# Moving the pieces of a block's end to other frames in a two-layer graph attention kernel

## The chip, the cores and the metric

The kernel runs on one core of one Trainium2 chip. Such a core has five engines with queues of their own: TensorE (matmuls; PE in the profile, its weight loads PEld), VectorE (DVE), ScalarE (ACT), GpSimd (POOL) and SyncE (SP), which issues most DMAs. The metric is the time of one execution on the device in microseconds, lower is better; the figure compared is the median of several runs.

## The reference

Input is x (8 batches, 2048 nodes, 256 features) and an adjacency matrix (2048 x 2048, 0 or 1). All arithmetic is 32-bit floating point. Two layers follow each other, each with a layer norm and a relu ahead of it and a residual around it.

- Layer 0: h = relu(norm(x)); q, k, v are projections of h, 4 heads of 64. The 2048 keys are split into 8 chunks of 256. Logits are clipped to -10 and 10, set to -10 where there is no edge, and the softmax is taken **within each chunk**; the 8 results are added. Then comes an output projection, plus h as residual, a layer norm with gamma and beta, and x is added.
- Layer 1: h = relu(norm(x)) W; the attention logit of nodes i and j is leaky_relu(src_i + dst_j), masked by the edges, with a softmax over all 2048; relu of the weighted sum of h, added to x.

## The kernel before, in words

**Tiling.** The queries of a batch are split in 4 blocks of 512 (nb = 0 to 3, in the code also zero, low, mid and last). A step is one block with one chunk of 256 keys, so a batch has 32 steps, 8 to a block. In a step TensorE makes the logits of 4 head tiles (L411), VectorE clips them and applies the edges in one instruction (clip, L451), ScalarE takes the exponential (L460), GpSimd adds two halves of the exponentials (add, L466), TensorE sums them over the keys (sums, L439) and multiplies the exponentials with v (values, L427). ScalarE turns the sums into 1/sum by a logarithm and an exponential (invert, L471 and L472), VectorE multiplies the numerators by it (scale, L481, into ctxT in a block's first step and into `prod`, of one buffer, in the others), and a DMA issued by GpSimd adds prod to ctxT (gather, L486).

**Frames.** The order of all instructions is written out by hand, and every engine runs its own in that order. A loop over frames f = 2 to 34 puts parts of four steps side by side: in frame f the logits of step f-1, the values of steps f-2 and f-3, the sums of step f-2, the scaling and gather of step f-3. A frame has two halves, `begin` and `end`, numbered n = 2f and 2f+1. Other work is hung into half frames as pieces: `todo[n]` lists what goes with n. Pieces without a mark run late: those of an even n in `end`, after clip 2 and **before** exponentials 1 and 2; those of an odd n in the same `end`, **after** these exponentials, just before the next frame begins with invert. Pieces marked first, pe, pe1 or mid have places of their own. SyncE's queue also holds the no-ops (`fence`) that order two groups of matmuls in one bank.

In what follows the frame of a step is the time from the first sums matmul of that step to that of the next step; it holds the end of one loop frame and most of the following one. A piece at n = 2f is issued around the sums of step f-2.

**A block's end.** When the 8 steps of block nb are done, `Between` makes the block's output. `beside()` gives its pieces with offsets from the block's end, n = (nb+1) x 16 + offset, for blocks 0, 1 and 2; block 3 comes at the end of the attention, outside of `beside()`. The pieces: `load` fetches x of the block (SP, 512 KB, L153); `residual` makes relu(norm(x)) again for two tiles (2 ScalarE ops, L293, tag hn, five buffers); `bias` adds bo to it (GpSimd, L665); `output_tiled` is the projection on TensorE (L635), `take_tiles` adds the residual (VectorE, L650); `stats` are mean and variance of one tile of 128 rows (VectorE, L270 and L271); `power` makes 1/sqrt (3 small ScalarE ops, L275 to L277), `shift` multiplies it by the mean (GpSimd, L281), `scaled` applies both to four tiles (4 ScalarE ops, L679); `gamma` and `beta` multiply and add (GpSimd, L685, L689); `add` adds the result to x (GpSimd, L693). After that `stats1`, `power1`, `shift1` do the norm of layer 1. Pieces with offsets of 16 and more stand beside early pieces of the next block.

**Around it.** In batch 0 the frames also hold the rest of the adjacency (8 searches on VectorE, L213, and conversions on ScalarE, L231, whose int tiles share the tag of x, four buffers). In the last frames of a batch the next batch's projections begin. Between the attentions of two batches TensorE runs layer 1 of the one and the projections of the other (L865, L355, L369).

Of the kernel before, what the change touches and what calls it, by code (L numbers as in the profile page):

```python
# [28 lines left out]
def gnn_two_layers(  # L29
# [26 lines left out]
    TB = NB // P  # L56
    NNB = N // NB
# [101 lines left out]
    def first(piece):  # L159

        piece.kind = "first"
        return piece

    def pe(piece):

        piece.kind = "pe"
        return piece

    def pe1(piece):
        piece.kind = "pe1"  # L170
        return piece

    def mid_clips(piece):
        piece.kind = "mid"
        return piece
# [418 lines left out]
    class Between:  # L594
# [150 lines left out]

        def beside(self):

            todo = {
                -3: [self.load],
                3: [lambda: self.residual(0)],  # L750
                4: [lambda: self.residual(1)],
                5: [lambda: self.bias(0)],
                6: [lambda: self.bias(1)],
                8: [pe(lambda: self.output_tiled(0)), lambda: self.stats([0]), lambda: self.beta(0)],
                9: [
                    pe1(lambda: self.output_tiled(1)), mid_clips(lambda: self.take_tiles(0)),
                    mid_clips(lambda: self.take_tiles(1)), lambda: self.stats([1]),
                ],
                10: [lambda: self.stats([2]), lambda: self.beta(1)],
                11: [lambda: self.stats([3])],  # L760
                12: [self.power],
                13: [self.shift],
                14: [lambda: self.scaled(range(TB))],
                15: [lambda: self.gamma(0)],
                16: [lambda: self.gamma(1)],
                18: [lambda: self.add(0)],
                20: [lambda: self.add(1)],
            }

            def at(n, *pieces):  # L770
                todo.setdefault(n, []).extend(pieces)

            if self.nb == NNB - 2:
                return todo
            at(22, lambda: self.stats1([0]))

            at(25, first(lambda: self.stats1([1, 2, 3])))
            at(26, self.power1)
            at(27, self.shift1)
            if self.nb == 1:  # L780
                at(28, lambda: self.norm1(0))
                at(29, lambda: self.norm1(1))
            return todo
# [501 lines left out]
```

The softmax here doesn't subtract the row's maximum and nothing guards it: scores larger than these inputs give would overflow.

## Time and profile before

| what | value |
|---|---|
| median of 3 runs | 3623.25 us (3621.5 to 3624.46) |
| the profiled execution: time | 3624.46 us |
| the profiled execution: span | 3622.7 us |
| TensorE clock granted | 0.998 |
| attention of one batch (from the first step's sums to the last's) | 251.4 to 264.0 us |
| from there to the next batch's first sums | 187.0 us in all but one case |

| group | count | mean ns |
|---|---|---|
| clip, L451 DVE | 1024 | 1220 |
| exponential, L460 ACT | 1024 | 1050 |
| add, L466 POOL | 512 | 2406 |
| scale, L481 DVE into prod | 448 | 685 |
| 1/sum, L471 and L472 ACT | 256 each | 597 and 630 |
| residual of blocks, L293 ACT, from x and krn | 128 | 586 |
| scaled, L679 ACT | 128 | 588 |
| bias L665, gamma L685, beta L689, add L693, POOL | 64, 48, 64, 48 | 1522, 1578, 1563, 1569 |
| gather, L486 POOL | 224 | 859, and 4.8 us (median) to its landing |

An instruction is named by its line, its engine and the tiles that it writes and reads. A row of the timeline has the start and the length in us; "x2" joins two instructions of one kind. What stands in square brackets is how long the engine was idle before, and whose signal ended that. A chain of instructions that ended last is part 4 of the page; part 3 lists the DMA queues with packets, megabytes and share. Two ScalarE ops that follow each other overlap a little, so that two residual ops take 1.06 us and four of L679 take 2.06.

### The profile page before, as it was taken

What the parts mean: (1) busy time and instruction counts of PE and PEld (TensorE: products, weight loads), DVE (VectorE), ACT (ScalarE), POOL (GpSimd) and SP (SyncE); (2) the same over time, 40 slices, a digit from 0 to 9 for tenths busy, and PEclk for the clock granted to TensorE, in tenths of its full rate; (3) what the DMA queues carried; (4) which work ended last, traced back from release to release, by engine and by line L of the source; (5) the groups of instructions that cost most, each with busy time, mean ns of one, the idle gap of its engine ahead of it and who ended that gap; (6) DMA issues with size and microseconds to landing.
All of it is one profiled execution on the core that took longest, in us unless ns stands there. A gap on an engine that the chain in (4) does not pass through costs nothing.

```text
span 3622.7 us, 104823 instructions
## 1 busy us (share of the span) xinstructions
PE 3587.4 (99%) x46544; PEld 2202.7 (61%) x46544; DVE 2580.6 (71%) x3967; ACT 1960.9 (54%) x2975; POOL 1788.1 (49%) x1138
## 2 busy tenths in 40 slices
PE   8999999999999999999999999999999999999999
PEld 4444785547744577555775558744586455865568
DVE  5887577866777667786677766677576785757866
ACT  5677416774167732676326772367723677137650
POOL 0678016870178702786027850378503784047831
PEclk9999999999999999999999999999999999999999
DMA  6444213341133412343113432144322343114321
GB/s 223 114 109 100 49 56 84 84 107 35 64 81 83 107 35 68 84 96 83 53 50 84 104 74 62 48 85 99 71 61 59 78 96 73 53 48 92 75 60 44
DMA packets 149431, 283.62 MB, mean 78 GB/s; under 512 B 39664, under 2 KB 104944, under 8 KB 140784
## 3 DMA queue, kind: packets, MB, share of 16 engines
q0 software_dynamic: 32256, 117.45, 17.6%
q1 hardware_dynamic: 100080, 157.36, 13.5%
q8 instruction: 364, 5.96, 0.7%
q10 hardware_dynamic: 16640, 2.10, 0.4%
q14 instruction: 91, 0.75, 0.1%
HBM read 138.41 MB, written 21.02 MB: 44 GB/s over the span
## 4 chain that ended last, share of the span: by engine, by line
PE 96%; DMA 2%; ACT 1%; DVE 1%; issue 0%; POOL 0%; ACTq 0%; SPq 0%; DVEq 0%; POOLq 0%
PE ps_s L411 24%; PE ps_n L427 24%; PE ps_s L865 12%; PE ps_t L439 6%; PE ps_n L865 6%; PE ps_t L865 6%; PE ps_t L635 2%; PE ps_t L355 2%; PE ps_n L355 2%; PE ps_s L355 2%; PE ps_t L723 2%; PE ps_n L723 1%; PE ps_t L369 1%; PE ps_n L369 1%; PE ps_t L302 1%; DMA ctxT<-prod 1%
## 5 line engine op out<-in xcount | busy, mean ns | idle before, releaser
L466 POOL TENSOR_TENSOR both<-e 128x1024 f32<-128x1024 f32 x512 | 1217.8, 2406 | 641.1 <-PE ps_t L439 353.3
L451 DVE SCALAR_TENSOR_TENSOR e<-ps_s,bound 128x1024 f32<-128x1024 f32 x1024 | 1223.9, 1220 | 401.4 <-PE ps_s L411 398.6
L411 PE MATMUL ps_s<-q,k 64*32 64x512 f32 x16384 | 1435.0, 590 | 2.1 <-DVE e L451 2.1
L460 ACT ACTIVATE e<-e 128x1024 f32<-128x1024 f32 x1024 | 1050.5, 1050 | 524.8 <-DVE e L451 505.1
L427 PE MATMUL ps_n<-e,v 64*32 64x512 f32 x16384 | 1220.2, 590 | 2.7 <-ACT e L460 2.1
L427 PEld LDWEIGHTS ps_n<-e,v 64*32 64x32 f32 x16384 | 453.9, 107 | 476.4 <-issue 396.4
L411 PEld LDWEIGHTS ps_s<-q,k 64*32 64x32 f32 x16384 | 451.8, 106 | 472.0 <-issue 326.9
L883 POOL TENSOR_TENSOR x<-x,r 128x256 f32<-128x256 f32 x124 | 95.8, 773 | 1107.2 <-DVE rz L875 1000.7
L439 PE MATMUL ps_t<-both,ones 64*32 64x512 f32 x4096 | 534.7, 591 | 0.1
L865 PE MATMUL ps_s<-g,w 128*128 128x257 f32 x2048 | 448.5, 380 | 0.0
L865 PEld LDWEIGHTS ps_s<-g,w 128*128 128x128 f32 x2048 | 389.4, 190 | 56.5
L481 DVE TENSOR_TENSOR prod<-ps_n,rz 128x512 f32<-128x512 f32 x448 | 288.3, 685 | 159.3 <-PE ps_n L427 96.4
L848 DVE SCALAR_TENSOR_TENSOR w<-bound,w 128x1024 f32<-128x1024 int8 x256 | 313.7, 1225 | 8.7
L865 PE MATMUL ps_n<-g,w 128*128 128x257 f32 x1024 | 292.4, 382 | 0.0
L865 PE MATMUL ps_t<-g,w 128*128 128x257 f32 x1024 | 289.8, 380 | 0.0
L842 DVE TENSOR_SCALAR w<-src,cd 128x512 f32<-128x512 f32 x512 | 265.2, 560 | 10.7 <-ACT src L836 6.9
L471 ACT ACTIVATE rz<-ps_t 128x512 f32<-128x512 f32 x256 | 152.8, 597 | 175.7 <-PE ps_t L439 136.9
L486 POOL DMA_DIRECT2D ctxT<-prod x224 | 192.3, 859 | 57.7 <-DVE prod L481 55.2
L865 PEld LDWEIGHTS ps_n<-g,w 128*128 128x128 f32 x1024 | 192.8, 190 | 44.3 <-issue 17.6
L865 PEld LDWEIGHTS ps_t<-g,w 128*128 128x128 f32 x1024 | 193.8, 189 | 28.2
L275 ACT ACTIVATE krn<-mv,eps 128x4 f32<-128x4 f32 x32 | 9.5, 296 | 292.7 <-DVE mv L271 292.7
L439 PEld LDWEIGHTS ps_t<-both,ones 64*32 64x32 f32 x4096 | 115.2, 106 | 85.8 <-SPq L383 42.4
(126 smaller groups left out, 3005.0 us busy)
## 6 DMA issues: line engine op xcount, KB each, us to landing
ctxT<-prod POOLq DMA_DIRECT2D x224, 512.0 KB, 4.8
bound<-bound_d SPq DMA_DIRECT2D x62, 1024.0 KB, 5.7
xp<-in_x_dram SPq DMA_DIRECT2D x60, 512.0 KB, 5.7
rows<-in_adj_dram SPq DMA_DIRECT2D x32, 512.0 KB, 5.2
x<-in_x_dram SPq DMA_DIRECT2D x32, 512.0 KB, 4.6
out_dram<-x SPq DMA_DIRECT2D x31, 512.0 KB, 2.9
src<-source_d SPq DMA_DIRECT2D x24, 256.0 KB, 4.8
bound_d<-bound_part ACTq DMA_DIRECT2D x16, 128.0 KB, 4.4
```

The costliest lines, as they stand in the source:

```text
L355: nc.tensor.matmul(pp, w[:, di, do * P:(do + 1) * P], self.hT[nb][:, di, :], start=di == 0, stop=di == FC - 1,)
L411: nc.tensor.matmul(self.s[n, o][c * Q:(c + 1) * Q, kt, :], self.k[p][rows, at:at + Q], self.q[p][rows, nb * NB:(nb + 1) * NB], start=True, ...
L427: made.append(nc.tensor.matmul(self.num[n, c][h * Q:(h + 1) * Q, :], self.v[rows, j * KT + kt, at:at + Q], self.e[n, p][rows, i * KT + kt, :],
L439: nc.tensor.matmul(self.total[n][h * Q:(h + 1) * Q, :], ones[rows, :], self.both[n, h // 2][rows, h % 2, :], start=half == 1, stop=half == 0,)
L451: nc.vector.scalar_tensor_tensor(self.e[n, p][:, i * KT:(i + 1) * KT, :], self.s.pop((n, o)), -CLIP * SC, bounds[nb][:, j * KT:(j + 1) * K ...
L460: nc.scalar.activation(e, e, AF.Exp, scale=1.0 / SC)
L466: nc.gpsimd.tensor_tensor(self.both[n, p], e[:, 0], e[:, 1], op=ALU.add)
L481: nc.vector.tensor_tensor(dst[:, c, :], self.num.pop((n, c)), self.rz[n], op=ALU.mult)
L486: nc.gpsimd.dma_start(self.ctxT[nb], self.prod.pop(n), accum_op=ALU.add)
L842: nc.vector.tensor_scalar(w[:, i, :], self.src[nb], self.cd[:, 0, j:j + 1], self.cd[:, 1, j:j + 1], op0=ALU.mult, op1=ALU.max,)
L848: nc.vector.scalar_tensor_tensor(two, bounds1[nb][:, j - 1:j + 1, :], 0.0, two, op0=ALU.is_gt, op1=ALU.mult)
L865: nc.tensor.matmul(accs[t][:, 0:F + 1], w[:, i, t * P:(t + 1) * P], g[:, j, :], start=j == 0, stop=j == NT - 1,)
```

## The change

Only the table of `beside()` is edited, the offsets at which pieces are hung into the half frames. x is loaded 6 half frames earlier; the two residual pieces go from 3 and 4 to -6 and -5, the two bias pieces from 5 and 6 to -4 and -2. The fourth tile of statistics, power, shift and scaled and the first gamma go one half frame later each. The second gamma goes from 16 to 18 and the two adds from 18 and 20 to 20 and 22; in block 2 (`soon`), whose end meets the end of the attention, they go to 17, 18 and 20. output_tiled, take_tiles, beta and the norm of layer 1 stay.

```diff
         def beside(self):
 
+            soon = int(self.nb == NNB - 2)
             todo = {
-                -3: [self.load],
-                3: [lambda: self.residual(0)],
-                4: [lambda: self.residual(1)],
-                5: [lambda: self.bias(0)],
-                6: [lambda: self.bias(1)],
+                -9: [self.load],
+                -6: [lambda: self.residual(0)],
+                -5: [lambda: self.residual(1)],
+                -4: [lambda: self.bias(0)],
+                -2: [lambda: self.bias(1)],
                 8: [pe(lambda: self.output_tiled(0)), lambda: self.stats([0]), lambda: self.beta(0)],
                 9: [
                     pe1(lambda: self.output_tiled(1)), mid_clips(lambda: self.take_tiles(0)),
                     mid_clips(lambda: self.take_tiles(1)), lambda: self.stats([1]),
                 ],
                 10: [lambda: self.stats([2]), lambda: self.beta(1)],
-                11: [lambda: self.stats([3])],
-                12: [self.power],
-                13: [self.shift],
-                14: [lambda: self.scaled(range(TB))],
-                15: [lambda: self.gamma(0)],
-                16: [lambda: self.gamma(1)],
-                18: [lambda: self.add(0)],
-                20: [lambda: self.add(1)],
+                12: [lambda: self.stats([3])],
+                13: [self.power],
+                14: [self.shift],
+                15: [lambda: self.scaled(range(TB))],
+                16: [lambda: self.gamma(0)],
+                18 - soon: [lambda: self.gamma(1)],
+                20 - 2 * soon: [lambda: self.add(0)],
+                22 - 2 * soon: [lambda: self.add(1)],
             }
```

## The prediction

> **What bounds the kernel now.** I read the page first, then the attention stretches one by one, then the timelines of the engines inside one frame. In this page's first and fourth part and its list of queues, TensorE is busy all the time and carries the chain; the third line is used further down.
>
> ```profile
> PE 3587.4 (99%) x46544; PEld 2202.7 (61%) x46544; DVE 2580.6 (71%) x3967; ACT 1960.9 (54%) x2975; POOL 1788.1 (49%) x1138
> ...
> q8 instruction: 364, 5.96, 0.7%
> ...
> PE 96%; DMA 2%; ACT 1%; DVE 1%; issue 0%; POOL 0%; ACTq 0%; SPq 0%; DVEq 0%; POOLq 0%
> ```
>
> A change that moves no TensorE work can only alter how long TensorE stands still. Its matmuls are pipelined, so such stops don't show as idle time; they show as longer frames. The next lines are busy times by stretch for the attention of batches 1 to 6, from the first matmul of the first step's row sums to that of the last (columns: window, length, busy time of PE, PEld, DVE, ACT, POOL, clock, DMA).
>
> ```profile
> 549.22:805.65 256.43, 256.43 (x4832) 128.22 (x4820) 198.50 (x237) 183.64 (x243) 200.35 (x118) 1.00 0.40 92
> 992.69:1251.79 259.10, 258.97 (x4833) 127.99 (x4821) 198.51 (x237) 184.30 (x243) 200.54 (x118) 1.00 0.40 91
> 1438.81:1694.68 255.87, 255.87 (x4833) 128.89 (x4820) 198.58 (x237) 184.18 (x243) 200.45 (x118) 1.00 0.41 92
> 1886.50:2143.07 256.57, 256.30 (x4833) 129.70 (x4820) 198.77 (x237) 183.86 (x243) 200.60 (x118) 1.00 0.41 92
> 2330.10:2588.44 258.34, 258.12 (x4833) 127.78 (x4821) 198.47 (x237) 183.68 (x243) 200.24 (x118) 1.00 0.40 91
> 2775.46:3034.08 258.62, 258.62 (x4832) 128.43 (x4820) 198.61 (x237) 184.38 (x243) 200.29 (x118) 1.00 0.40 91
> ```
>
> The same work takes 255.87 to 259.10 us. Against the shortest, the six lose 0.56 + 3.23 + 0 + 0.70 + 2.47 + 2.75 = 9.7 us. A clean frame is 7.72 us (the sums' first matmul at 646.54, then at 654.27 and 661.99). All that shorter stops could give, with batches 0 and 7 and about 1 us left in the best batch, is some 20 us of 3623.
>
> What makes the losses? Frame by frame, nearly every long one has a late scaling of the numerators on VectorE (prod, L481). One clean frame, and two in which it waits (start, length, idle before and releaser):
>
> ```profile
> 658.36 1.29 DVE L481 TENSOR_TENSOR prod<-ps_n,rz 128x512 f32<-128x512 f32 x2
> ...
> 577.70 1.29 DVE L481 TENSOR_TENSOR prod<-ps_n,rz 128x512 f32<-128x512 f32 x2 [1.01 <-DMA ctxT<-prod]
> ...
> 1029.80 1.29 DVE L481 TENSOR_TENSOR prod<-ps_n,rz 128x512 f32<-128x512 f32 x2 [1.35 <-DMA ctxT<-prod]
> ```
>
> prod has one buffer, and the accumulating DMA of the step before ("gather", L486) still reads it. Measured from the frame's mark (its first sums matmul), the scaling ends at +5.38 in the clean frame, +6.51 and +6.75 in the others; those two frames are 0.58 and 0.83 us too long. So TensorE stops when the scaling ends after about +5.93; the slack is 0.55 us. The gather is issued at +7.1 and lands 4.5 to 6.7 us later.
>
> Is a late issue, from GpSimd pieces, to blame? The two pieces of one frame, on GpSimd:
>
> ```profile
> 677.50 1.58 POOL L693 TENSOR_TENSOR x<-x,o 128x512 f32<-128x512 f32 x1
> 678.75 1.57 POOL L665 TENSOR_TENSOR hn<-hn,bo_r 128x512 f32<-128x512 f32 x1
> 680.00 5.02 POOL L466 TENSOR_TENSOR both<-e 128x1024 f32<-128x1024 f32 x2
> 684.71 1.55 POOL L665 TENSOR_TENSOR hn<-hn,bo_r 128x512 f32<-128x512 f32 x1
> ```
>
> The adds end at 685.0, about 0.1 us later than in other frames, and no gather follows: this is the block's first step, which writes ctxT directly. The doubled frame costs nothing; its frame is 7.72 us. With one piece GpSimd idles 0.84 us before the adds. In the frames after the first stop of a block the gather starts at +7.05 to +7.15, pieces or not: the lateness is in the transfer.
>
> **What the Trainium skill says.** "DMA: Bandwidth & Descriptors", section "Queues, rings and completion order": each DMA engine takes turns between its queues, a packet at a time. "Perfetto Trace Analysis", section "The 4-stage abstract model": an instruction has 64 bytes. The trace agrees: (46544 + 46544) x 64 B = 5.96 MB, the instruction queue's total in 364 packets of 16 KB. These are TensorE's instructions. In batch 3 the gathers that landed in 4.5 us had mostly no such packet in their window; the one of 6.7 us at 1031.4 has one, and no packet of a load. The program as built has 24068 TensorE instructions before and after, so these collisions stay in their frames. "PSUM — Partial Sum Buffer", section "Engine vs sequencer instructions": the queues of ScalarE, VectorE and GpSimd are strict FIFO; the timelines agree, so a moved piece delays all behind it.
>
> **The change, part by part.** It concerns three block ends in each of 8 batches, 24 in all; no instruction's work is added or removed.
>
> *x load (L153), SP, three frames earlier.* It was issued 1.3 us into the frame of step 3, 11 or 19, over the landing of the gather before: in step 2 these take 5.17 to 5.48 us, against 4.49 to 5.19 in step 1. It now goes with steps 0, 8, 16, where no later scaling waits for a gather in flight (step 8 and 16 use ctxT). In step 0 it shares the time with a 1 MB bounds load that is wanted five frames later; nothing waits on SP before it. With 4.8 us the stop at step 3 goes: 0.58, 0.62, 1.08, 0.58, 0.70 us in batches 1, 2, 4, 5, 6. But step 4's gather (5.21 us in batch 1) or 3's (6.22 in 2) then makes much the same stop itself, since TensorE is still ahead by the amount. I keep about 0.9 us of batch 4 and 0.1 of four others: **-1.3 us**; bounds 0 and -7 us (all stops of steps 3 to 6).
>
> *Residual (two ACT ops, 1.06 us) and bias (1.5 us of POOL) before the block end.* Both residual pieces now fall into one frame, one ahead of the second exponentials, one behind them. Ahead there are 1.5 us free (ACT ends at 652.0, clip 1 releases at 653.5), or 0.8 with the 0.7 us of power1 beside it once a batch: at most 0.3 late. Behind there are 0.87 us free. Both are hidden by the scaling's 0.55 us: 0. A second buffer pair of hn is held longer; five are there. Bias: one piece a frame, 2.05 us with the shift, where 2.4 fit: 0.
>
> *Statistics one frame later (0.6 us of DVE), stats1 unmoved.* The frame that loses it lets VectorE wait for TensorE as it is (0.17 us before a clip), so 0. In batch 0 a frame gets it beside a search (1.21 us), and another two residuals beside two keeps (2.04 us of ACT): **+0.4 us**, bounds 0 and 1.5.
>
> *The scaling by ScalarE (L679, 4 ops, 2.06 us): from an even half frame to an odd one.* This is the step that I expect to decide. An even piece stands before exponentials 1 and 2, an odd one behind them and before 1/sum (L471). Batch 1, ScalarE, start and length:
>
> ```profile
> 645.80 2.19 ACT L460 ACTIVATE e<-e 128x1024 f32<-128x1024 f32 x2 [0.79 <-DVE e L451]
> 648.86 0.60 ACT L471 ACTIVATE rz<-ps_t 128x512 f32<-128x512 f32 x1 [0.87 <-PE ps_t L439]
> ...
> 650.02 1.99 ACT L460 ACTIVATE e<-e 128x1024 f32<-128x1024 f32 x2
> 651.92 2.06 ACT L679 ACTIVATE o<-o,rn 128x256 f32<-128x256 f32 x4
> 653.89 1.99 ACT L460 ACTIVATE e<-e 128x1024 f32<-128x1024 f32 x2
> 656.64 0.60 ACT L471 ACTIVATE rz<-ps_t 128x512 f32<-128x512 f32 x1 [0.77 <-PE ps_t L439]
> ```
>
> Before, it fits into the long gap. After, exponentials end at +1.45, the four ops at +3.48, L471 starts at +3.41 instead of +2.35 (the ops overlap by 0.1). L472 ends at +4.68 (both take 1.27), the two scalings at +5.97: 0.04 over. The third exponential ends 2.21 after L471's start, at +5.62; the matmuls that read it start at +5.47:
>
> ```profile
> 659.74 0.61 PE L427 MATMUL ps_n<-e,v 64*32 64x512 f32 x4
> ```
>
> That is 0.15 us, for blocks 0 and 1 of 8 batches: 16 x 0.15 = **+2.4 us**, bounds 0 and 0.3 each. In block 2 the frame starts later for ScalarE (the exponentials end at 789.28), L471 goes from 790.20 to 791.35 and the scalings end at 793.84 instead of 793.18, 0.55 over. Some of it returns: in batch 2 that frame is 0.26 longer than in batch 1 and the next 0.26 shorter. 0.36 x 8 = **+2.9 us**, bounds 0.1 and 0.6 each. Cover gone altogether, the price would be the full 1.06 us of L471's delay.
>
> *gamma, add, power, shift on their new places:* one POOL piece a frame, 0. In block 2 both gammas share a frame and delay the last adds by 0.7 us, to 803.35; their reader starts at 805.65: 0.
>
> **Sum:** -1.3 + 0.4 + 2.4 + 2.9 = +4.4 us. The profiled execution has a span of 3622.7 and a time of 3624.46, 1.2 above the median 3623.25; the span's addition goes to the median: 3627.5 us, +0.12%. Within 0.2% (7.2 us) is about what a measurement of this kernel can't tell from no change.
>
> **Rivals.** *The delay of ScalarE isn't hidden (slower, 0.25).* If L471's shift of 1.06 us meets only the scaling's 0.55 us, each of 24 ends costs 0.51: +12.2, with the rest (-0.9) 3634.5; it decides from 0.3 us an end on. For it: the chain L471, L472, scaling has no other gap. Against: the scaling ended at +5.35. *The gathers recover (faster, 0.08).* The early load frees all of steps 3 to 6, 7 us, and the ACT step costs nothing: 3616 or below. Against: instruction packets remain. *Nothing shows (part of the 0.67 for no change).* Both effects hidden: 3623. That the order doesn't change is excluded by the built program: the pieces stand elsewhere in all queues.
>
> **Range.** Costs at their lower ends with half the rival's gain: 3617; upper ends (16 x 0.3 + 8 x 0.6 + 1.5 = 11) and some more: 3637.
>
> **What will show it.** Right: L679 directly before L471 with no idle time between; L471 at +3.4 of its frame; the frames of steps 13 and 21 at 7.8 to 8.0 us; step 3's stop moved to a later step; bad batches 2, 5, 6 still bad. Wrong: attention stretches near 255 us everywhere (the load was the cause), or frames of steps 13, 21 over 8.1 us.

## The result and the profile after

The changed kernel is slower: 3639.61 us (median of 6 runs, 3634.25 to 3644.45) against 3622.38 us before (6 runs, 3618.75 to 3624.59). The ratio is 1.0042, with an interval from 1.0032 to 1.0053. I had forecast 3627.5 us in a range of 3617 to 3637, and the likeliest case as no difference that can be measured. Not +4.4 but +17.2 us came out, above the range.

The profiled execution took 3641.61 us with a span of 3639.8, 17.1 longer than that of before. From its page, the first and fourth part and the row of the scaling:

```profile
PE 3603.3 (99%) x46544; PEld 2221.9 (61%) x46544; DVE 2581.9 (71%) x3967; ACT 1958.7 (54%) x2975; POOL 1788.7 (49%) x1138
...
PE 96%; ACT 1%; DVE 1%; DMA 1%; issue 0%; POOL 0%; ACTq 0%; SPq 0%; DVEq 0%; POOLq 0%
...
L481 DVE TENSOR_TENSOR prod<-ps_n,rz 128x512 f32<-128x512 f32 x448 | 288.4, 686 | 182.6 <-PE ps_n L427 87.0
```

VectorE, ScalarE and GpSimd do the same work in the same time (2580.6, 1960.9 and 1788.1 us before); TensorE is "busy" 15.9 us longer with the same 46544 matmuls. The scaling's idle time rose from 159.3 to 182.6 us. Busy times by stretch for the attention of batches 1 to 6, with the columns of the same view of before:

```profile
555.83:815.38 259.55, 259.46 (x4832) 130.15 (x4820) 198.54 (x237) 183.71 (x243) 199.57 (x118) 1.00 0.40 90
1002.41:1262.49 260.08, 259.66 (x4832) 131.97 (x4820) 198.45 (x237) 183.92 (x243) 199.80 (x118) 1.00 0.40 90
1449.52:1707.61 258.09, 257.81 (x4833) 131.83 (x4820) 198.78 (x237) 183.76 (x243) 199.54 (x118) 1.00 0.40 91
1895.30:2153.49 258.19, 257.91 (x4832) 130.31 (x4820) 198.71 (x237) 183.81 (x243) 199.75 (x118) 1.00 0.40 91
2340.52:2601.06 260.54, 259.69 (x4833) 129.02 (x4820) 198.40 (x237) 183.73 (x243) 199.77 (x118) 1.00 0.40 90
2788.09:3047.73 259.64, 259.19 (x4833) 131.62 (x4820) 198.52 (x237) 183.80 (x243) 199.73 (x118) 1.00 0.40 90
```

Every one is longer than its counterpart, by 1.0 to 3.1 us. Over all eight batches the attention grew by 20.1 us, of which batch 0 has 6.9. The stretch between the attentions of batches 3 and 4 fell from 191.83 to 187.69; in the eleven profiles of this study it lies anywhere from 187.0 to 191.9, so its fall can't be put down to the change. Start and end differ by another 1.1: 20.1 - 4.1 + 1.1 = 17.1 us.

Frame by frame (frame of a step after minus before, sums over the eight batches, us; the steps left out make +0.4):

| steps | sum | what stands there |
|---|---|---|
| 1 | +4.6 | batch 0 alone, +4.81 |
| 2 to 7 | -0.9 | load of x moved away |
| 10, 18, 26 | -1.3 | fewer pieces in a block's frames |
| 13, 14, 15 | -0.5, +3.5, +0.9 | the frame of the odd `scaled` of block 0, and the two after it |
| 21, 22, 23 | +0.8, +8.0, +0.9 | the same for block 1 |
| 29, 30 | +2.4, +1.2 | the same for block 2 |

The loss is where I had looked for it, around `scaled`, but one frame later. The frames of steps 13 and 21 themselves are clean (7.72 us) in most of batches 1 to 7; those of 14 and 22 are up to 1.5 us too long.

**Where it comes from, in batch 1.** The frame of step 13 begins at 661.37, that of step 14 at 669.09 and that of step 15 at 677.95; times with a plus are counted from a frame's begin. ScalarE, changed kernel (start, length):

```profile
662.72 2.06 ACT L679 ACTIVATE o<-o,rn 128x256 f32<-128x256 f32 x4
664.69 0.57 ACT L471 ACTIVATE rz<-ps_t 128x512 f32<-128x512 f32 x1
665.30 0.63 ACT L472 ACTIVATE rz<-rz 128x512 f32<-128x512 f32 x1
665.83 1.99 ACT L460 ACTIVATE e<-e 128x1024 f32<-128x1024 f32 x2
```

L471 starts at +3.32 without a pause, as forecast (+3.41). The third exponential, the first of the last row, ends at about 666.9. Now GpSimd in the same time, first in the changed kernel, then in the kernel before (its frame of step 13 begins at 654.27):

```profile
663.76 2.39 POOL L466 TENSOR_TENSOR both<-e 128x1024 f32<-128x1024 f32 x1 [0.71 <-PE ps_t L439]
667.00 2.40 POOL L466 TENSOR_TENSOR both<-e 128x1024 f32<-128x1024 f32 x1 [0.85 <-POOL both L466]
669.33 0.87 POOL L486 DMA_DIRECT2D ctxT<-prod  x1
```

```profile
656.66 4.74 POOL L466 TENSOR_TENSOR both<-e 128x1024 f32<-128x1024 f32 x2 [0.84 <-PE ps_t L439]
661.32 0.88 POOL L486 DMA_DIRECT2D ctxT<-prod  x1
```

Before, the two adds run back to back and the gather goes out at +7.05. After, GpSimd stands idle for 0.85 us between them (the releaser named is GpSimd itself; the second add starts 0.1 us after the third exponential's end), and the gather, queued behind the add, goes out at +7.96. For what follows, VectorE, the DMA's own view, and TensorE (its weight loads, and the first sums matmul of step 15):

```profile
665.96 1.29 DVE L481 TENSOR_TENSOR prod<-ps_n,rz 128x512 f32<-128x512 f32 x2 [0.47 <-ACT rz L472]
...
674.86 1.29 DVE L481 TENSOR_TENSOR prod<-ps_n,rz 128x512 f32<-128x512 f32 x2 [1.31 <-DMA ctxT<-prod]
```

```profile
ctxT<-prod POOLq DMA_DIRECT2D x1, 512.0 KB, 5.4
```

```profile
675.61 0.15 PEld L427 LDWEIGHTS ps_n<-e,v 64*32 64x32 f32 x8 [0.86 <-DVE prod L481]
...
677.95 0.61 PE L439 MATMUL ps_t<-both,ones 64*32 64x512 f32 x4
```

In step 13 the scaling ends at +5.88, still within the slack. But prod was free for the next step only at 669.33 + 5.42 = 674.75, so step 14's scaling ends at +7.06; TensorE waits for it, and that frame is 1.14 us too long. The two scalings take 1.29 us, begin 0.11 us after the landing and must end by +5.93, so a gather has to land by +4.5 of the next frame. Issued at +7.05 it may take 5.2 us, issued at +7.96 only 4.3, and none of the 224 takes less than 4.46. So **every gather behind a late add stops TensorE**, by about its duration minus 4.3. (For the gathers of about 4.5 us a second path, shown below, would cost as much.) Batches 1 to 7, gather of step 13 and frame of step 14 (us over 7.72):

| batch | 1 | 2 | 3 | 4 | 5 | 6 | 7 |
|---|---|---|---|---|---|---|---|
| issue to landing | 5.42 | 4.54 | 4.50 | 5.10 | 5.52 | 4.53 | 4.50 |
| minus 4.3 | 1.12 | 0.24 | 0.20 | 0.80 | 1.22 | 0.23 | 0.20 |
| frame of step 14, excess | 1.14 | 0.19 | 0.25 | 0.83 | 1.26 | 0.32 | 0.24 |

### The profile page after: what moved, and what is told of

Same layout as the page of the kernel before. It is cut to its first block, busy times and chain, and to the rows that moved or that the text cites. A ratio compares the mean times of both kernels' runs of the same rounds, so it can differ in the third digit from the quotient of the medians.

```text
span 3639.8 us, 104788 instructions
## 1 busy us (share of the span) xinstructions
PE 3603.3 (99%) x46544; PEld 2221.9 (61%) x46544; DVE 2581.9 (71%) x3967; ACT 1958.7 (54%) x2975; POOL 1788.7 (49%) x1138
## 3 DMA queue, kind: packets, MB, share of 16 engines
q1 hardware_dynamic: 100080, 157.36, 13.6%
## 4 chain that ended last, share of the span: by engine, by line
PE 96%; ACT 1%; DVE 1%; DMA 1%; issue 0%; POOL 0%; ACTq 0%; SPq 0%; DVEq 0%; POOLq 0%
PE ps_n L427 24%; PE ps_s L411 24%; PE ps_s L866 12%; PE ps_t L439 7%; PE ps_n L866 6%; PE ps_t L866 6%; PE ps_t L635 2%; PE ps_t L355 2%; PE ps_n L355 2%; PE ps_s L355 2%; PE ps_n L723 2%; PE ps_t L723 2%; PE ps_t L369 1%; PE ps_n L369 1%; PE ps_t L302 1%; PE ps_n L302 1%
## 5 line engine op out<-in xcount | busy, mean ns | idle before, releaser
L427 PEld LDWEIGHTS ps_n<-e,v 64*32 64x32 f32 x16384 | 463.9, 107 | 473.4 <-issue 367.8
L411 PEld LDWEIGHTS ps_s<-q,k 64*32 64x32 f32 x16384 | 464.3, 106 | 466.4 <-issue 316.9
L439 PE MATMUL ps_t<-both,ones 64*32 64x512 f32 x4096 | 546.8, 592 | 0.5
L481 DVE TENSOR_TENSOR prod<-ps_n,rz 128x512 f32<-128x512 f32 x448 | 288.4, 686 | 182.6 <-PE ps_n L427 87.0
L843 DVE TENSOR_SCALAR w<-src,cd 128x512 f32<-128x512 f32 x512 | 265.1, 560 | 10.7 <-ACT src L837 6.9
L471 ACT ACTIVATE rz<-ps_t 128x512 f32<-128x512 f32 x256 | 152.1, 594 | 152.5 <-PE ps_t L439 112.9
```

Of the source, the lines that this page charges most:

```text
L411: nc.tensor.matmul(self.s[n, o][c * Q:(c + 1) * Q, kt, :], self.k[p][rows, at:at + Q], self.q[p][rows, nb * NB:(nb + 1) * NB], start=True, ...
L427: made.append(nc.tensor.matmul(self.num[n, c][h * Q:(h + 1) * Q, :], self.v[rows, j * KT + kt, at:at + Q], self.e[n, p][rows, i * KT + kt, :],
L439: nc.tensor.matmul(self.total[n][h * Q:(h + 1) * Q, :], ones[rows, :], self.both[n, h // 2][rows, h % 2, :], start=half == 1, stop=half == 0,)
L481: nc.vector.tensor_tensor(dst[:, c, :], self.num.pop((n, c)), self.rz[n], op=ALU.mult)
L843: nc.vector.tensor_scalar(w[:, i, :], self.src[nb], self.cd[:, 0, j:j + 1], self.cd[:, 1, j:j + 1], op0=ALU.mult, op1=ALU.max,)
```

## The experiments

Each ratio below is to runs of the kernel before on the same chip in the same session; their medians are 3621.06 us for the first two groups, 3621.56 for the next three and 3624.96 for the last. The theory: the late add on GpSimd makes the gather late, and this costs most; batch 0's step 1 is a second, separate fault. The rivals: the early half of the change (load, residual, bias) is to blame; ScalarE's delay stops TensorE directly, without the gather; a later chain costs as such, wherever it stands.

### Each half of the change alone

`chain_alone` is the changed kernel with the early half taken back, and `ahead_alone` the kernel before with the early half alone:

```diff
-                -9: [self.load],
-                -6: [lambda: self.residual(0)],
-                -5: [lambda: self.residual(1)],
-                -4: [lambda: self.bias(0)],
-                -2: [lambda: self.bias(1)],
+                -3: [self.load],
+                3: [lambda: self.residual(0)],
+                4: [lambda: self.residual(1)],
+                5: [lambda: self.bias(0)],
+                6: [lambda: self.bias(1)],
```

> The change without its earlier half: load, residual and bias stay where they were; only stats, power, shift, scaled, gamma and add stand on their new places. Theory (the four ops of L679 delay L471, the third exponential and with it the add on GpSimd by about 1 us, and the gather queued behind that add lands too late for the next frame's scaling): frames of steps 14 and 22 are 0.2 to 1.3 us longer than before, as in the changed kernel, step 29 about 0.37 longer, 14 to 17 us in all: 3636 to 3640 us against 3622 before; batch 0's frame of step 1 as before (about 7.7 us). Rival (the loss comes from load, residual and bias ahead of the block's end): within 3 us of before.

> The other half alone: load, residual and bias early, everything from stats on where it was. Theory: batch 0's frame of step 1 is 12.5 us, 4.8 longer than before, since the second load of a_r is queued behind the load of x on SyncE; steps 14, 22 and 29 are as before; step 3's stops are gone or moved: 3622 to 3627 us. Rival (the early half makes the gathers late): 3633 us or more, with long frames in steps 14 and 22.

`chain_alone`: 3635.34 us, ratio 1.0034 (1.0021 to 1.0047). Its frames repeat those of the changed kernel: steps 13 to 15 +3.5 us in all, 21 to 23 +10.7, 29 and 30 +3.6; step 1 as before. `ahead_alone`: 3622.58 us, ratio 0.9999 (0.9991 to 1.0007). Its profiled execution took 3614.39 us, 8 below its median. In it steps 2 to 7 gave 2.5 us back, more than the 0.9 of the whole change. Step 22 was still 2.3 us longer, which I hadn't expected: the gathers that it waits for took 5.65 to 6.14 us in five batches. Why is open; in `scaled_even`, which holds the same early half, step 22 isn't longer. And batch 0's step 1 was **not** long in this profile (7.72 us), against what I had expected; see below. The slowdown is the late chain's.

### Taking away the wait for the gather

prod has one buffer of 4 KB. But hT, which the norms of layer 1 use, has two of the same size and is idle for nearly all of the attention. One tag with three buffers serves both, in the same space. Both kernels were run with this:

```diff
-                self.hT[nb] = work.tile([P, FC, NB], F32, tag="hT", name="hT")
+                self.hT[nb] = work.tile([P, FC, NB], F32, tag="hT", name="hT", bufs=3)
...
-                self.prod[n] = work.tile([P, 2, NB], F32, tag="prod", name="prod", bufs=1)
+                self.prod[n] = work.tile([P, 2, NB], F32, tag="hT", name="prod", bufs=3)
...
-                self.hT = work.tile([P, FC, NB], F32, tag="hT", name="hT")
+                self.hT = work.tile([P, FC, NB], F32, tag="hT", name="hT", bufs=3)
```

> The kernel before, with prod sharing the buffers of hT: one tag of three 4 KB buffers instead of two for hT and one for prod, so that a scaling no longer waits for the gather of the step before. Theory (nearly all losses of the attention are scalings that wait for a gather): no L481 has a wait on the DMA ctxT<-prod, attention stretches of batches 1 to 6 all within about 1 us of each other at 254 to 256, and 3600 to 3611 us. Rival (the gathers are late together with something else that also stops TensorE, such as the collision of the instruction queue itself): 3618 us or more.

> The changed kernel with the same three buffers shared by prod and hT. Theory (late gather as the cause): the add on GpSimd and the gather are still about 0.9 us late in steps 13 and 21, but steps 14 and 22 are clean (7.72 to 7.8 us); what is left above before_prod3 is batch 0's step 1 (4.8 us) and step 29 (0.37 in 8 batches, 3 us), about 5 to 9 us: 3607 to 3619 us. Rival (the delay of ScalarE stops TensorE by itself, through L471, the scaling or the third exponential): steps 14 and 22 stay long, and it is 15 us or more above before_prod3.

`before_prod3`: 3603.88 us, ratio 0.9949 (0.9937 to 0.9961). The list of what ended the idle time before L481 has no DMA left, which made 38.8 us in 50 waits in the kernel before (us, times):

```profile
  PE ps_n L427: 116.1, 86
  ACT rz L472: 6.1, 2
  issue: 5.6, 19
  DVE e L451: 0.3, 1
```

The stretches of batches 2 and 6, which had 259.10 and 258.62 us before:

```profile
989.36:1244.45 255.09, 255.09 (x4832) 125.30 (x4820) 198.89 (x237) 183.96 (x243) 200.26 (x118) 1.00 0.41 92
...
2760.43:3015.69 255.26, 255.26 (x4833) 137.69 (x4820) 198.75 (x237) 183.94 (x243) 200.26 (x118) 1.00 0.41 92
```

Batches 1 to 6 now all lie at 255.09 to 255.26 us. So nearly all of their difference came from gathers that landed late.

`after_prod3`: 3613.10 us, ratio 0.9977 (0.9968 to 0.9986), 9.2 us above `before_prod3`, just over the 5 to 9 forecast, instead of the 17.2 that the change cost with one buffer. GpSimd is as late as in the changed kernel. This is its frame of step 13 in batch 1, which begins at 655.69 (the next at 663.49), and below it TensorE's weight loads at the begin of step 14:

```profile
661.45 2.41 POOL L466 TENSOR_TENSOR both<-e 128x1024 f32<-128x1024 f32 x1 [0.86 <-POOL both L466]
663.79 0.85 POOL L486 DMA_DIRECT2D ctxT<-prod  x1
```

```profile
663.49 0.11 PEld L439 LDWEIGHTS ps_t<-both,ones 64*32 64x32 f32 x2 [0.26 <-issue]
663.91 0.11 PEld L439 LDWEIGHTS ps_t<-both,ones 64*32 64x32 f32 x2 [0.31 <-POOL both L466]
```

The gather goes out at +8.10 and takes 5.8 us, and still the frame of step 14 is 8.03 us, 0.31 too long, where it was 1.14. What is left has another reader: the sums themselves. The add ends at 663.86, after the frame's begin, and TensorE waits 0.31 us for it. Steps 14 and 22 are 0.23 to 0.31 long in nearly all batches here; I had expected them clean. So the late add has two readers that TensorE waits for: its sums, and through GpSimd's queue the gather. Over the whole run the sums' wait for the add makes 7.9 us in 26 times here and 1.6 in 6 in `before_prod3`. With one buffer both readers are at work in the changed kernel; its list of waits has both (waiting, released by: us, times, longest). The kernel before has 59.1 us in 167 times for the first and 1.1 in 3 for the second:

```profile
PEld ps_n L427 <- DVE prod L481: 74.5, 195, 1.3
...
PEld ps_t L439 <- POOL both L466: 7.0, 26, 0.6
```

Of the 10.9 us by which the attention of `after_prod3` exceeds that of `before_prod3`, steps 13, 14, 22 and 23 make 4.6, steps 29 and 30 make 2.8 and batch 0's step 1 makes 3.1. So ScalarE's delay costs 7.4 us without any gather, and some 10 of the chain's 17 in the changed kernel's frames went through the gather.

### The place of scaled

One thing in the changed kernel is moved, into the even half frame; in the other run, scaled is cut in two:

```diff
-                15: [lambda: self.scaled(range(TB))],
-                16: [lambda: self.gamma(0)],
+                16: [lambda: self.scaled(range(TB)), lambda: self.gamma(0)],
```

```diff
-                15: [lambda: self.scaled(range(TB))],
-                16: [lambda: self.gamma(0)],
-                18 - soon: [lambda: self.gamma(1)],
+                15: [lambda: self.scaled([0, 1])],
+                17: [lambda: self.scaled([2, 3]), lambda: self.gamma(0)],
...
+            at(18 - soon, lambda: self.gamma(1))
```

> The changed kernel with one thing moved: scaled goes on from offset 15 to 16, into the even half frame, so that its four ops stand before exponentials 1 and 2, where they stood in the kernel before, but a frame later. Theory (the place behind the exponentials and right before L471 is what costs): L471 starts at about +2.35 of every frame, the adds are not late, steps 14 and 22 lose at most what ahead_alone loses there, step 29 is as before: 3617 to 3627 us. Rival (a later chain as such costs, since gamma and add move to other frames with it): 3632 us or more.

> The changed kernel with scaled cut in two: two tiles at offset 15 and two at 17, both in odd half frames, gamma behind them. Theory (the price depends on how long ScalarE is held before L471): two ops take about 1.03 us after exponentials that end at +1.45, so L471 starts at about +2.5 instead of +3.4, the adds are at most 0.2 us late and the gathers are issued at about +7.2; steps 14 and 22 are within 0.5 us of before: 3618 to 3629 us. Rival (any ops in an odd half frame delay the add): steps 14 and 22 stay 0.6 us or more longer, 3632 us or more.

`scaled_even`: 3621.61 us, ratio 1.0003 (0.9994 to 1.0012): the whole loss is gone, though every piece of the chain is as late as in the change or later. ScalarE in its frame of step 14, which begins at 663.43:

```profile
661.14 2.07 ACT L679 ACTIVATE o<-o,rn 128x256 f32<-128x256 f32 x4
663.11 1.99 ACT L460 ACTIVATE e<-e 128x1024 f32<-128x1024 f32 x2
665.81 0.60 ACT L471 ACTIVATE rz<-ps_t 128x512 f32<-128x512 f32 x1 [0.70 <-PE ps_t L439]
```

Ahead of the exponentials the four ops fit into a gap, and L471 starts at +2.38 after 0.70 us of idle time. `scaled_split`: 3624.06 us, ratio 1.0009 (1.0001 to 1.0017); steps 14 and 22 together 1.0 us over before instead of 11.4. With two ops in the odd half frame L471 starts at +2.38, not late at all (I had expected +2.5), and the second add starts at +4.74 as in a clean frame. So two ops are free there and four aren't: it is a question of the slack, not of the half frame as such. That a later chain costs by itself is refuted.

### The load of x ahead of a_r, in batch 0

```diff
-                -9: [self.load],
+                -8 if self.nb + self.proj.b == 0 else -9: [self.load],
```

> The changed kernel with the load of x of block 0 in batch 0 one half frame later, so that it stands behind the second load of a_r on SyncE. Theory: a_r lands no later than 6 us after its issue, all four ops of layer1_vector take 0.42 us and end before GpSimd's add begins, and batch 0's frame of step 1 is 7.7 us instead of 12.5: 3634 to 3637 us. Rival (step 1 was long from something else, for instance the clip or the rows of the adjacency): it stays at 10.8 us or more.

In the changed kernel SyncE issued, in batch 0's first step:

```profile
100.90 0.41 SPq L153 DMA_DIRECT2D xp<-in_x_dram  x1
101.38 0.53 SPq L153 DMA_DIRECT2D x<-in_x_dram  x1
102.08 0.37 SPq L987 DMA_DIRECT2D a_r<-in_L_gnn_a_dram  x1
```

The x load of 512 KB is new ahead of the second a_r, which lands 7.6 us after its issue; before it took 4.6. VectorE's four products with it, and GpSimd's add beside them:

```profile
108.28 0.42 DVE L990 SCALAR_TENSOR_TENSOR prod<-w1s,a_r 128x256 f32<-128x256 f32 x1
...
109.78 0.43 DVE L990 SCALAR_TENSOR_TENSOR prod<-w1s,a_r 128x256 f32<-128x256 f32 x1 [1.08 <-DMA a_r<-in_L_gnn_a_dram]
...
110.13 2.59 DVE L990 SCALAR_TENSOR_TENSOR prod<-w1s,a_r 128x256 f32<-128x256 f32 x1
...
112.66 2.34 DVE L451 SCALAR_TENSOR_TENSOR e<-ps_s,bound 128x1024 f32<-128x1024 f32 x2
```

```profile
110.06 2.38 POOL L466 TENSOR_TENSOR both<-e 128x1024 f32<-128x1024 f32 x1 [2.99 <-PE ps_t L439]
```

The wait is 1.08 us, but the last product then takes 2.59 us instead of 0.42: it began 0.07 us after GpSimd's add and ended 0.28 us after it. The clips behind it are over 3 us late, and the frame is 4.8 us longer. Not all of that is the product's. In `after_prod3` TensorE stands still for the same 1.8 us there, and the frame is 3.1 us longer. In the changed kernel the clock granted to TensorE fell behind the stop: its records show it halved from 115.8 to 119.2 us, in `after_prod3` they don't. Busy times by stretch, with the columns of the table of the attentions, first the changed kernel, then `after_prod3`:

```profile
116.00:119.00 3.00, 3.00 (x40) 1.10 (x32) 2.30 (x3) 1.15 (x2) 2.40 (x2) 0.50 0.05 10
```

```profile
115.00:118.00 3.00, 3.00 (x64) 1.20 (x56) 2.95 (x4) 1.51 (x3) 2.63 (x2) 1.00 0.00 0
```

Half the clock for 3.4 us loses 1.7 us, the difference of the two frames. Why it fell in one of them is open. Every one of the eleven profiles has at least one such stretch of 3.4 us; the three whose time between batches 3 and 4 is longest (191.8 to 191.9 us) have one there, and near the end the changed kernel has 6.8 us at half the clock where the kernel before has 3.4.

`load_after_ar` has no such wait: a_r takes 4.6 us, all products 0.42, step 1 is 7.72 us. Its time is 3637.22 us, ratio 1.0039 (1.0027 to 1.0052), which can't be told from the changed kernel's 1.0042: only the profiles show the gain. As for `ahead_alone`: where x stands ahead of a_r, a_r lands after 5.9 to 6.0 us in three profiles (`ahead_alone`, `scaled_even`, `scaled_split`), with a step 1 of 7.7 us, and after 7.6 us in three (the changed kernel, `after_prod3`, `xp_early`), with one 0.9 to 4.8 us longer. What decides between the two landings is open. So this is a fault that costs up to 3.1 us in some executions, and 4.8 with the slower clock.

### The loads beside the gather in step 22

Step 22 lost 8.0 us, step 14 only 3.5. In step 22 the two loads of the next batch's x are issued while the late gather is under way.

```diff
-            at(STEPS2 - 14, lambda: ahead.load(0))
-            at(STEPS2 - 13, lambda: ahead.load(1))
+            at(STEPS2 - 14 - 2 * (b > 0), lambda: ahead.load(0))
+            at(STEPS2 - 13 - 2 * (b > 0), lambda: ahead.load(1))
```

> The changed kernel with the two loads of the next batch's x one frame earlier in batches 1 to 6 (in batch 0 their buffers are not free by then). Theory (in step 22 a late gather is also slowed by these two loads, which are issued within 2 us of it): the gather issued in step 21 lands in 4.5 to 5.2 us instead of 5.5 to 5.8, and the frame of step 22 falls from 8.9 to 9.3 us to 8.0 to 8.6 in batches 2, 3, 4 and 6; some of it comes back in step 21: 3633 to 3639 us. Rival (the loads don't matter, the lateness of the issue alone does): step 22 stays at 8.9 us or more.

The gathers of step 21 in batches 2, 3, 4 and 6 fell from 5.51, 5.54, 5.67 and 5.54 us to 4.56, 4.48, 5.15 and 4.55, and the frames of step 22 from 8.89, 8.98, 9.12 and 8.94 us to 8.06, 7.97, 8.61 and 7.72. In batch 0, whose loads stayed, step 22 kept its 9.0 us. Over all batches step 22 lost 4.6 us less and step 21 took 0.9 back. So the loads lengthen the late gather. The time is 3634.88 us, ratio 1.0036 (1.0023 to 1.0050), again too near to the changed kernel's to be told from it. Batch 7, which loads nothing, had shown the same in the changed kernel: 4.54 us and a frame of 7.97.

### The change mended, with the gather's wait gone

The edits of `scaled_even`, `load_after_ar` and `after_prod3` together:

> The changed kernel with its two faults mended and the gather's wait gone: scaled at offset 16, batch 0's first load of x behind a_r, and prod in the three buffers shared with hT. Theory (the rest of the change moves only work that is hidden): attention stretches of batches 1 to 6 at 254.8 to 255.2 us, as in before_prod3 at 255.09 or a few tenths shorter, and a time within 3 us of before_prod3: 3600 to 3607 us. Rival (one piece a frame on GpSimd and early residuals give slack that pays once no gather waits): 3598 us or less.

3602.43 us, ratio 0.9941 (0.9927 to 0.9955); two of its stretches:

```profile
987.86:1242.74 254.88, 254.88 (x4833) 123.96 (x4821) 198.97 (x237) 183.53 (x243) 199.29 (x118) 1.00 0.40 91
1429.77:1684.64 254.87, 254.87 (x4832) 124.18 (x4820) 198.98 (x237) 183.57 (x243) 199.26 (x118) 1.00 0.40 91
```

They are 0.21 us shorter than in `before_prod3`, three frames of 0.07 us in each batch. This can't be told in the time: the intervals of the two overlap for the most part. Both beat the kernel before by 0.5 to 0.6%, and nearly all of it is the buffers' doing.

## Why the prediction was wrong

**The step that failed is "The scaling by ScalarE (L679, 4 ops, 2.06 us)".** Its first half was right: L679 directly before L471 with no idle time, L471 at +3.32 (forecast +3.41), the scaling's end at +5.88 (forecast +5.97), within the slack. I then charged the late third exponential, at +5.62, only with the matmuls that read it (0.15 us). It has a second reader, the second add on GpSimd, which starts at +4.73 in the frame of before. There the exponential ends 2.21 us after an L471 at +2.37, at +4.58, so the slack was 0.15 us at most. L471 came 0.95 us later, and 0.90 of it reached the add (+5.63) and then the gather (+7.96 instead of +7.05). My text had most of what was needed: the two adds in a row, the gather's issue at +7.1, landings from 4.5 us up, and that a gather which lands late delays the next frame's scaling. I had even asked whether a late issue is to blame, and answered it for GpSimd's pieces alone, not for the add. The term of 2.4 us for blocks 0 and 1 was 13.6 in the changed kernel's frames of steps 13 to 15 and 21 to 23. The 0.15 us at the matmuls didn't show: with L471 at +3.32 the exponential ends at +5.51 instead of +5.62, and these frames stayed at 7.72 in five batches of step 13.

**Block 2 was right:** +2.9 us forecast, 0.37 us in six of eight batches and 2.4 in all in step 29. There the scaling itself ends at +6.38, 0.45 over the limit (0.55 forecast), and the 0.37 stays with three buffers. Step 30's +1.2 us, nearly all in batch 7, wasn't forecast.

**The load of x** moved step 3's stops to later steps, as forecast. Its gain of -0.9 us in steps 2 to 7 (-1.3 forecast) isn't shown: in the six profiles with one buffer and the early load these steps range from -2.5 to +0.4 us against before, and `chain_alone`, without it, has +1.1. And "nothing waits on SP before it" was wrong in batch 0, where a_r's second load stands behind it. I had looked at the bounds, which share the time with x, and not at the entry that the load was moved past in its own queue.

**Hidden edits:** outside of batch 0, and but for the open 2.3 us of `ahead_alone`'s step 22, residual, bias, gamma and the adds cost nothing that the profiles show, as forecast; in step 10 the frames even came out 0.07 us shorter in all batches. Batch 0's +0.4 us has its counterpart in step 12, +0.55 here. It isn't the statistics beside a search: `chain_alone`, which moves them, has -0.03 there, and `ahead_alone`, which moves the residuals and not them, +0.52. With the residuals beside ScalarE's conversions L471 starts at +3.51 instead of +2.82 in step 11, the second add at +5.83 instead of +5.25, and the gather lands late for step 12. This is the path of `scaled` once more, so that the size was right by luck.

**The rivals:** the slower one, 3634.5 us at a chance of 0.25, was nearest in the time, but its mechanism, L471 and the scaling within the same frame at 0.51 us an end, isn't what happened in blocks 0 and 1. My sign for "wrong", frames of steps 13 and 21 over 8.1 us, looked one frame too early. The remark that shorter stops hold some 20 us was right: `before_prod3` took 17 of them. One sum of the range doesn't come out: half of the faster rival's 7 us gives a lower end of about 3620 us, not 3617.

## What to carry to other kernels

When a piece delays an instruction, list all its readers, on every engine, and for each what is queued behind it there; a reader with the least slack (here 0.15 us at most, on GpSimd) passes the delay on even where the path that you look at absorbs it. A DMA that frees a single buffer carries a delay into the next iteration, so look for the cost one frame after the cause. And where a stop hangs on such a buffer, look for tiles of the same size that are idle at that time: sharing their buffers cost no space and was worth more here than any order of the pieces that was tried.

## What the runs showed of the hardware

I hadn't expected VectorE's product of two SBUF inputs to take 2.59 us instead of 0.42 beside an add of GpSimd (and 2.63 in `after_prod3`, again till 0.29 us after the add's end), while the clips, which read one input from PSUM, take their 1.22 us beside the same adds. The Trainium skill, "SBUF — State Buffer", section "Who interferes with whom", says it: a VectorE instruction with two SBUF inputs contends with a GpSimd instruction that reads SBUF, the pair of ports that they share is an exclusive lock, and the order of issue decides who is blocked. The runs fit this from both sides: above, the product that began after the add ended after it. In `xp_early` product and add begin within 0.01 us of each other; VectorE on the first row, GpSimd on the second:

```profile
107.39 0.42 DVE L990 SCALAR_TENSOR_TENSOR prod<-w1s,a_r 128x256 f32<-128x256 f32 x1
```

```profile
107.39 5.18 POOL L466 TENSOR_TENSOR both<-e 128x1024 f32<-128x1024 f32 x2 [2.98 <-PE ps_t L439]
```

Here the product kept its 0.42 us, and the two adds took 5.18 us instead of 4.74, longer by about that time. So VectorE's wait of 1.0 to 1.1 us for a_r cost 0.9 us in one execution and 3.1 in another, and 4.8 in a third, in which TensorE's clock was also halved for 3.4 us.
